# Transposes by strips through memory: the second layer's input in layer 0, and the query and key heads of three sequences, in a two-layer transformer kernel

## The chip, the cores and the metric

The kernel runs on one core of a Trainium2 chip, in one launch. The metric is the time on the device in microseconds (us). The kernel before takes 1124.99 us, the median of three runs (1124.24 to 1125.60). Everything is computed in 32-bit floats.

The engines are named as in the profile: PE (TensorE, matrix products; PEld is its loading of weights), DVE (VectorE), ACT (ScalarE), POOL (GpSimd) and SP (SyncE, which here only issues transfers). Each engine works through its own list of instructions in order, and waits in front of one whose inputs are not there. SP and ACT issue plain transfers (DMAs) in the same way, in order, POOL the gathers and scatters.

## The reference

`x` has 4 sequences of 1024 tokens with 256 features. Two layers follow each other:

```python
xn = _layernorm(x)
x = x + attention0(xn) + ffn0(xn)        # layer 0
xn = _layernorm(x)
x = x + attention1(xn) + experts1(xn)    # layer 1
```

- `attention0` is causal, one head, 256 wide: softmax(q kT / 16) v over all earlier tokens, then a layer norm of (out + v) and a projection. `ffn0` is relu(xn W1 + b1) W2 + b2, 1024 wide.
- `attention1` is a gated unit: `qk = silu(ln(xn) Wqk + bqk)` is 64 wide; four heads come of it by a scale, an offset and a rotation by position (`rope`): quad_q, lin_q, quad_k, lin_k. Within groups of 64 tokens, relu(quad_q quad_kT / 64 + bias) squared weighs `v`; beside it lin_q multiplies the sum over the sequence of lin_kT v, divided by n. Their sum is multiplied by a gate silu(ln(xn) Wg + bg), projected and normalised.
- `experts1` sends each token to the best 2 of 8 experts (softmax of xn Wg); each expert computes (silu(xn W1 + b1) * (xn W3 + b3)) W2 + b2, 512 wide, where W1, W2, W3 have low-rank corrections added. The two results are added with their weights.

## The kernel before

**Layer 0** runs in 16 units of 256 tokens, 4 per sequence (`u = 4b + p`; line 739 ff.). The iteration of unit `u` holds for PE: transposes of the nearest attention weights (`turns`, line 546), the first part of the hidden layer (`hidden`, `pm`, L539), the queries of unit u + 1 (L476), the transposes of `xl` of unit u - 1 (`norms_turn`, L636), the weighted sum `pz` (`weighted`, L571 near, L574 far), the logits of unit u - 1 (`pl`, L653), the scores of unit u + 1 (`sc`, L492), the rest of the hidden layer, then `finish` (`po` L590, `pv` L594), and a product of low-rank expert factors (`multiply`, L411 to L414), whose result is added to expert weights on DVE (L417) and stored by SP (`wm<-wt`, L418 and L420).

`xl` is the normalised input of layer 1, made on DVE by `norms` at the end of an iteration (L621). `norms_turn` makes `xlT` of it, with features on partitions: four PE transposes into PSUM and a copy by ACT (L641). Its products with the router's and the qk weights are made by `logits`. For sequences 1 to 3 SP stores `xlT` (`xld`) for later.

**Strips.** DVE can transpose blocks of 32 x 32, not across the 128 partitions. Some data is therefore turned by way of DRAM: it is stored, loaded again in four transfers of 32 partitions that bring the blocks to their places in runs of 32 numbers (128 bytes), and turned by one DVE instruction. The kernel before does so with `xn` of units above 2 (`strip`, lines 431 to 436, turned at L455) and with attention weights on tokens of earlier units. For the latter, `bands` (line 515) stores the weights of each half of a unit (`atd`, L519), loads the matching rows of `xn` in another order (`xn2`, L524, once per unit) and loads the weights as `band` (L529), turned at L566. They are called for units that are `far` (u > 1 and p > 0).

**Layer 1** begins with the attention of sequence 0 (about 500 to 560 us), then come 36 blocks of experts (32 of 256 tokens and 4 of 128, about 560 to 926 us), then the attention of sequences 1 to 3, with the gathers of the experts' results. In an experts' block PE runs `up` (32 products, L957) and, for the block before, `down` (16 products, L978). DVE makes `g` (L965), turns the next block's `xt` into `xT` (L945) and scales `yt` (L980). SP loads the weights of the block after next; `xt` comes through ACT's queue.

For a sequence of the attention, `heads` (line 1072) applies silu to `qk` on ACT and makes the four heads on DVE: per half sequence two instructions of 128x1024 (L1084, L1088) and six of 128x512 (L1097 to L1102), into `a.r`. `values` makes `v` (L1114, L1116, L1119). `groups` (line 1123) turns `a.r` by 16 PE transposes (L1134, L1135), copied by DVE (`qlT`, L1136) and ACT (`kkT`, L1137), and uses it: `plk` (L1143), `ps` (L1150), later `po` (L1207). `gated` makes gate and sum, `project` the projection (`pj`, L1232) and its norm, `combine` adds the experts' results (L1046).

**What sets the order.** A scheduler orders each engine's list from the order of the program and from its own estimates of when things are ready. `tc.issue_after(x)` keeps an instruction behind another one. `tile_pool`s are buffers, with `bufs` copies for each tag; a tile of a tag waits until the tile `bufs` earlier is no longer read.

Of the kernel before, what the change touches and what calls it, by code (L numbers as in the profile page):

```python
# [67 lines left out]
def block_kernel(ctx: ExitStack, tc: tile.TileContext, x, wq, wk, wv, wfc, w1, w2, wqk, wvl, wg,  # L68
# [107 lines left out]
    xnd = dram.tile([B * NP, 2 * P, D], F32, name="xnd")  # L176
    atd = dram.tile([B * NP, 2 * P, (NP - 1) * 2 * P], F32, name="atd")
    xld = [dram.tile([P, DC, N], F32, name=f"xld{b}") for b in range(B)]
# [59 lines left out]
    with ExitStack() as l0:  # L238
# [27 lines left out]
        early = act.tile([P, 3 * D], F32, tag="att", name="early", bufs=4)  # L266
# [126 lines left out]
        def merge(u, after):  # L393
# [13 lines left out]
            def multiply():  # L407
# [3 lines left out]
                nc.tensor.matmul(pa, f1[:, ts(c, P)], f1[:, D : D + HID], start=True, stop=True)  # L411
                nc.tensor.matmul(pb, f3[:, ts(c, P)], f3[:, D : D + HID], start=True, stop=True)
                for i in range(2):
                    nc.tensor.matmul(pc[:, i, :], f2[:, ts(2 * c + i, P)], f2[:, HID : HID + D],  # L414
                                     start=True, stop=True)
                for k, p in enumerate((pa, pb, pc.rearrange("p i d -> p (i d)"))):
                    nc.vector.tensor_tensor(wt[:, k, :], p, wt[:, k, :], ALU.add)  # L417
                nc.sync.dma_start(  # L418
                    out=wm13[e, :, 0:EB1].rearrange("p (k c w) -> p k c w", k=2, c=DC)[:, :, c, :], in_=wt[:, 0:2, :])
# [8 lines left out]
        def keep(u):  # L428
            nc.sync.dma_start(out=xnd[u].rearrange("(i p) d -> p i d", p=P), in_=xns[u])

        def strip(u):
            keep(u)
            w = strips[u] = act.tile([P, DC, 2 * P], F32, tag="strip", name="strip", bufs=1)
            src = xnd[u].rearrange("(i r) (c j a) -> j r c i a", r=32, c=DC, a=32)
            for j in range(4):
                nc.sync.dma_start(out=w[32 * j : 32 * j + 32].rearrange("r c (i a) -> r c i a", a=32), in_=src[j])


        def first(u):
# [9 lines left out]
            if u > 2:  # L449
                strip(u)  # L450
# [31 lines left out]
        def scores(u, qT):  # L482
            b, p = divmod(u, NP)
            atts = []
            for i in range(2):
# [11 lines left out]
                att = act.tile([P, N], F32, tag="att", name="att", bufs=4)  # L497
# [6 lines left out]
                if far(u):  # L504
                    bands(u, i, att)
# [9 lines left out]
        def bands(u, i, att):  # L515
# [10 lines left out]
            got = act.tile([P, N], F32, tag="att", name="band", bufs=4)[:, 0:w]  # L526
            src = there.rearrange("(i r) (j k) -> j r i k", r=32, j=4)
            for j in range(4):
                nc.sync.dma_start(out=got[32 * j : 32 * j + 32].rearrange("r (i k) -> r i k", i=4), in_=src[j])  # L529
            bands.got.append(got)  # L530

# [50 lines left out]
        def finish(u, hT, zT):  # L582
# [3 lines left out]
            for i in range(2):  # L586
# [6 lines left out]
                for c in range(DC):  # L593
                    nc.tensor.matmul(pv, zT[:, c, ts(i, P)], vo_s[:, c, :, :],  # L594
                                     start=(c == 0), stop=(c == DC - 1))
# [11 lines left out]
        def norms(u):  # L607
# [21 lines left out]
            return xl  # L629

        def norms_turn(u, xl):
            b, p = divmod(u, NP)
            pt = bank([P, DC, 2 * P], "pt")
            for i in range(2):
                for c in range(DC):
                    nc.tensor.transpose(pt[:, c, ts(i, P)], xl[:, i, ts(c, P)], ident)  # L636
# [4 lines left out]
            nc.scalar.copy(xlT, pt)  # L641
            if b:
                nc.sync.dma_start(out=xld[b][:, :, ts(p, 2 * P)], in_=xlT)
# [3 lines left out]
        def logits(u, xlT, lg):  # L647
# [3 lines left out]
            for i in range(2):  # L651
                for c in range(DC):
                    nc.tensor.matmul(pl[:, i, :], xlT[:, c, ts(i, P)], wqr_s[:, c, :],  # L653
                                     start=(c == 0), stop=(c == DC - 1))
# [77 lines left out]
        for u in range(U):  # L732
# [7 lines left out]
            if u == 1:  # L740
                for k in range(3):
                    keep(k)
                fold_second(raw)
# [17 lines left out]
            if u:  # L761
                xlT = norms_turn(u - 1, xl)
            zT = weighted(u, attT)
            if u:
                logits(u - 1, xlT, lgs)
# [18 lines left out]
            finish(u, hT, zT)  # L784
            if u + 1 < U:
# [20 lines left out]
    with ExitStack() as l1:  # L806
# [141 lines left out]
        def up(xT, w13, n):  # L948
            g = exp.tile([P, EC, n], F32, tag="g", name="g")
            for m2 in range(EC // 2):  # L950
# [9 lines left out]
                for j in range(2):  # L960
                    m = 2 * m2 + j
                    nc.scalar.activation(s[:, j, :], p1[:, j, :], AF.Silu, bias=w13[:, EB1 + m : EB1 + m + 1])  # L962
# [26 lines left out]
        def blocks(order, ahead):  # L989
            last = None  # L990
            xts, ws, xT = ahead
            for k, i in enumerate(order):
# [6 lines left out]
                if i == 3:  # L999
                    tokens.after = weights.last  # L1000
                    slots(up.g)
                    heads.after = up.g
                if k + 1 < len(order):
                    xT = turn(xts.pop(order[k + 1]), wide(order[k + 1]), up.early if i == 0 else None)
                if last is not None:
# [4 lines left out]
        def experts(ahead):  # L1010
# [7 lines left out]
            values.after = down.last  # L1018
# [52 lines left out]

        def heads(b):
            a = at[b]
            bt = ts(b, NT)
            with tc.issue_after(at[0].silu0 if b == 0 else at[0].link), tc.issue_after(route.exp):
                nc.scalar.activation(qk[:, bt, :], qk[:, bt, :], AF.Silu)
            a.r = mid.tile([P, NT, 4, QK], F32, tag="r", name="r")
            for h in range(NH):
                tt = slice(h * T, (h + 1) * T)
                nt = slice(b * NT + h * T, b * NT + (h + 1) * T)  # L1080
                shape = [P, T, 4, QK]
                hd = tmp.tile(shape, F32, tag="hd", name="hd")
                with tc.issue_after(heads.after) if b == 1 else nullcontext():
                    nc.vector.tensor_tensor(hd, qk[:, nt, :].unsqueeze(2).to_broadcast(shape),  # L1084
                                            hg_s[:, h].unsqueeze(1).to_broadcast(shape), ALU.mult)

                with tc.issue_after(a.pace[2]) if b == h == 0 else nullcontext():
# [294 lines left out]
```

## Time and profile before

| what | value |
|---|---|
| runs | 1124.99 us median (1124.24 to 1125.60) |
| profiled execution | 1128.42 us, of which the span from the first to the last instruction is 1126.7 |
| granted PE clock, mean | 0.998 of full speed |
| PE busy | 1106.9 us (98%) |
| DVE busy | 555.4 us (49%) |
| ACT busy | 288.7 us (26%) |
| plain transfers of SP (queue q1) | 137.89 MB, 37.9% of the 16 DMA engines' span |
| plain transfers of ACT (queue q10) | 18.10 MB, 7.5% |
| layer 0, 60 to 440 us | PE busy 380.00, DVE 184.16, DMA 0.45 |
| experts, 560 to 930 us | PE busy 369.64, DVE 141.53, DMA 0.69 |
| attention of sequences 1 to 3, 930 to 1127 us | PE busy 185.62, DVE 134.70, DMA 0.23 |

A line of the timeline gives start, length, engine, program line, operation, out<-in, shape, type and count. A PE record lasts from an instruction's start until its result is written; neighbours overlap, so the step from one start to the next is what an instruction takes in the queue. A line of the waits gives who waited for whom: us in total, times, longest.

### The profile page before, as it was taken

The numbers are of one execution on the slowest core, as the hardware profiler recorded it, in microseconds if no ns is written. First come the engines' busy times: TensorE is split into PE (matmuls) and PEld (weight loads), VectorE is DVE, ScalarE is ACT, GpSimd is POOL, SyncE is SP. The second block draws the span as 40 slices with busy tenths as digits, with TensorE's granted clock in tenths as the row PEclk, the third lists the DMA queues.
The fourth block names the chain that finished last, engine by engine and source line by source line (L and its number), as shares of the span: only waits on it lengthen the run. The fifth ranks groups of instructions, "written<-read, shape, count | busy, mean of one in ns | idle before, by whom it ended". The sixth has DMA issues, their size and how long they took to land. (4 is left out here: it accounts for less than half of the span.)

```text
span 1126.7 us, 15401 instructions
## 1 busy us (share of the span) xinstructions
PE 1106.9 (98%) x5132; PEld 867.4 (77%) x5132; DVE 555.4 (49%) x1533; ACT 288.7 (26%) x758; POOL 177.7 (16%) x216
## 2 busy tenths in 40 slices
PE   8999999999999999999999999999999999999997
PEld 6788888888888888774688888888888884655645
DVE  5444554455444454547575623322332326677946
ACT  3323333333323333225211111111111113121121
POOL 2200002222032114141000000000000004453410
PEclk9999999999999999999999999999999999999999
DMA  8735434553455334420648786777777621322301
GB/s 308 200 100 160 129 99 149 159 178 119 132 162 155 94 128 141 158 96 33 222 101 290 212 269 190 241 227 221 238 228 223 231 85 57 121 76 75 95 28 37
DMA packets 186801, 173.77 MB, mean 154 GB/s; under 512 B 113888, under 2 KB 156384, under 8 KB 181600
## 3 DMA queue, kind: packets, MB, share of 16 engines
q1 hardware_dynamic: 99216, 137.89, 37.9%
q10 hardware_dynamic: 81360, 18.10, 7.5%
q0 software_dynamic: 6144, 16.79, 4.5%
q8 instruction: 41, 0.67, 0.3%
q14 instruction: 40, 0.33, 0.1%
HBM read 122.78 MB, written 51.02 MB: 154 GB/s over the span
## 5 line engine op out<-in xcount | busy, mean ns | idle before, releaser
L957 PE MATMUL p<-xT,w 128*128 128x256 f32 (+1 forms) x1152 | 241.2, 368 | 0.0
L957 PEld LDWEIGHTS p<-xT,w 128*128 128x128 f32 x1152 | 209.4, 190 | 26.9 <-issue 0.3
L1036 POOL DMA_INDIRECT y<-yg,slot x64 | 65.3, 1021 | 491.0 <-DVE v L1116 421.2
L962 ACT ACTIVATE s<-p,w 128x256 f32<-128x256 f32 (+1 forms) x144 | 58.8, 459 | 314.3 <-PE p L957 228.4
L965 DVE SCALAR_TENSOR_TENSOR g<-p,w,s 128x256 f32<-128x256 f32 (+1 forms) x144 | 60.8, 463 | 159.1 <-PE p L957 156.8
L978 PE MATMUL py<-w,g 128*128 128x256 f32 x544 | 123.4, 379 | 0.0
L539 PE MATMUL pm<-xnT,w_s 128*128 128x256 f32 x512 | 118.5, 379 | 0.0
L590 PE MATMUL po<-w_s,hT 128*128 128x256 f32 x512 | 116.1, 380 | 0.0
L978 PEld LDWEIGHTS py<-w,g 128*128 128x128 f32 x544 | 102.9, 190 | 14.2 <-DVE g L965 0.3
L590 PEld LDWEIGHTS po<-w_s,hT 128*128 128x128 f32 x512 | 96.9, 190 | 20.1 <-issue 8.0
L539 PEld LDWEIGHTS pm<-xnT,w_s 128*128 128x128 f32 x512 | 95.6, 192 | 11.6
L714 POOL DMA_INDIRECT xg<-xr,put x64 | 63.9, 998 | 209.0 <-ACT hT L542 138.2
L492 PE MATMUL sc<-xnT,qT 128*128 128x256 f32 (+1 forms) x320 | 65.8, 361 | 0.0
L542 ACT ACTIVATE hT<-pm,colt 128x256 f32<-128x256 f32 x128 | 53.9, 466 | 42.2 <-PE pm L539 42.2
L1114 PE MATMUL pv<-wvl_s,xl 128*128 128x512 f32 x128 | 58.1, 599 | 3.4 <-DVE v L1116 3.1
L594 PE MATMUL pv<-vo_s,zT 128*128 128x512 f32 x128 | 60.1, 592 | 0.0
L1232 PE MATMUL pj<-wo_s,gd 128*128 128x256 f32 x256 | 57.0, 381 | 2.6 <-DVE o L1234 2.1
L492 PEld LDWEIGHTS sc<-xnT,qT 128*128 128x128 f32 x320 | 54.6, 191 | 6.0 <-ACT qT L479 0.2
L1185 PE MATMUL pg<-xl,wg_s 128*128 128x512 f32 x128 | 57.5, 593 | 0.0
L1232 PEld LDWEIGHTS pj<-wo_s,gd 128*128 128x128 f32 x256 | 48.0, 190 | 10.2 <-DVE o L1234 3.3
L980 DVE TENSOR_TENSOR yt<-py,w 128x512 f32<-128x512 f32 (+1 forms) x36 | 23.8, 662 | 59.0 <-PE py L978 59.0
L603 DVE SCALAR_TENSOR_TENSOR x<-pv,rs,x 128x256 f32<-128x256 f32 x32 | 15.5, 484 | 72.1 <-ACT rs L189 47.7
(256 smaller groups left out, 1351.8 us busy)
## 6 DMA issues: line engine op xcount, KB each, us to landing
w<-wm SPq DMA_DIRECT2D x36, 1028.0 KB
w<-wm SPq DMA_DIRECT2D x36, 640.0 KB
wt<-in_ew_dram SPq DMA_DIRECT2D x16, 768.0 KB
wm<-wt SPq DMA_DIRECT2D x16, 512.0 KB
xt<-xg ACTq DMA_DIRECT2D x128, 64.0 KB
yg<-yt ACTq DMA_DIRECT2D x32, 256.0 KB
xnd<-xn SPq DMA_DIRECT2D x16, 256.0 KB
wm<-wt SPq DMA_DIRECT2D x16, 256.0 KB
```

Source lines behind the costliest of these rows:

```text
L492: nc.tensor.matmul(sc[:, kp * 2 * P : kp * 2 * P + w], qT[:, c, ts(i, P)], xnTs[b * NP + kp][:, c, 0:w], start=(c == 0), stop=(c == DC - 1))
L539: nc.tensor.matmul(pm[:, j, :], w1_s[:, c, ts(2 * m2 + j, P)], xnTs[u][:, c, :], start=(c == 0), stop=(c == DC - 1))
L590: nc.tensor.matmul(po[:, i, :], hT[:, m, ts(i, P)], w2_s[:, m, :], start=(m == 0), stop=(m == IC - 1))
L594: nc.tensor.matmul(pv, zT[:, c, ts(i, P)], vo_s[:, c, :, :], start=(c == 0), stop=(c == DC - 1))
L714: w = nc.gpsimd.indirect_dma_start(out=xg, out_offset=bass.IndirectOffsetOnAxis(ap=put[:, b * NT + t : b * NT + t + 1], axis=0), in_=xrs[b ...
L957: nc.tensor.matmul(p[:, j, :], w13[:, w0 : w0 + P], xT[:, c, :], start=(c == 0), stop=(c == DC - 1))
L962: nc.scalar.activation(s[:, j, :], p1[:, j, :], AF.Silu, bias=w13[:, EB1 + m : EB1 + m + 1])
L965: up.g = nc.vector.scalar_tensor_tensor(g[:, m, :], p3[:, j, :], w13[:, EB3 + m : EB3 + m + 1], s[:, j, :], ALU.add, ALU.mult).ins
L978: down.last = nc.tensor.matmul(py[:, k, :], g[:, m, ts(k, P)], w2[:, m * D : (m + 1) * D], start=(m == 0), stop=(m == EC - 1)).ins
L1036: w = nc.gpsimd.indirect_dma_start(out=ys[b][:, t, k, :], out_offset=None, in_=yg, in_offset=bass.IndirectOffsetOnAxis(ap=slot[:, n : n + ...
L1114: nc.tensor.matmul(pv, a.xl[:, c, ts(t, P)], wvl_s[:, c, :], start=(c == 0), stop=(c == DC - 1))
L1232: nc.tensor.matmul(pj, a.gd[:, m, ts(n, P)], wo_s[:, m, :], start=(m == 0), stop=(m == HC - 1))
```

## The change

It has four parts.

1. **`xl` of sequences 0 to 2 (units 0 to 11) in strips.** `norms` stores `xl` in DRAM (`xlr`) and loads it in strips (`strip`, now for any tile). `norms_turn` turns it by one DVE instruction, kept behind the last scores of the iteration, in place of four PE transposes and an ACT copy. For the iterations u = 1 to 12 `norms_turn` and `logits` are called after `finish`, and `logits`' products come behind the last `pv`. Sequence 3 keeps the PE transposes.
2. **The heads of sequences 1 to 3** are made in the experts' blocks 5, 8, 11, 14, 17 and 20, half a sequence in each: silu behind that block's own (ACT), then the eight DVE instructions behind its `g`. ACT's queue stores the result (`rd`) in the next block. `heads_back` loads it in strips (`qs`, `ks`) and, for the linear keys, plainly (`rl`): ten loads of SP per sequence, those of sequence 1 behind the last expert weights. `groups` turns them by three DVE instructions in place of 16 PE transposes and four copies.
3. **Stores behind the fetches of attention weights.** The stores of `xn`, `xld` and `wm13` are kept behind the last `band` fetch issued so far (`bands.last`). `multiply`'s products are kept behind the last `pv`.
4. **Buffers.** The four buffers of `att`, which `band` shared, become two of `att` and two of `band`; `strip` has two buffers in place of one; the pools of the last stage stand in another order, and one of them (`tmp`) is gone.

```diff
-        def strip(u):
-            keep(u)
-            w = strips[u] = act.tile([P, DC, 2 * P], F32, tag="strip", name="strip", bufs=1)
-            src = xnd[u].rearrange("(i r) (c j a) -> j r c i a", r=32, c=DC, a=32)
+        def keep(there, rows):
+            with tc.issue_after(bands.last) if bands.last else nullcontext():
+                nc.sync.dma_start(out=there.rearrange("(i p) d -> p i d", p=P), in_=rows)
+
+        def strip(there, rows):
+            keep(there, rows)
+            w = act.tile([P, DC, 2 * P], F32, tag="strip", name="strip", bufs=2)
+            src = there.rearrange("(i r) (c j a) -> j r c i a", r=32, c=DC, a=32)
             for j in range(4):
                 nc.sync.dma_start(out=w[32 * j : 32 * j + 32].rearrange("r c (i a) -> r c i a", a=32), in_=src[j])
+            return w
...
                 for k, p in enumerate((pa, pb, pc.rearrange("p i d -> p (i d)"))):
                     nc.vector.tensor_tensor(wt[:, k, :], p, wt[:, k, :], ALU.add)
-                nc.sync.dma_start(
-                    out=wm13[e, :, 0:EB1].rearrange("p (k c w) -> p k c w", k=2, c=DC)[:, :, c, :], in_=wt[:, 0:2, :])
+                with tc.issue_after(bands.last) if bands.last else nullcontext():
+                    nc.sync.dma_start(
+                      out=wm13[e, :, 0:EB1].rearrange("p (k c w) -> p k c w", k=2, c=DC)[:, :, c, :], in_=wt[:, 0:2, :])
                 nc.sync.dma_start(out=wm2[e, :, ts(c, HID)], in_=wt[:, 2, :])
...
-            got = act.tile([P, N], F32, tag="att", name="band", bufs=4)[:, 0:w]
+            got = act.tile([P, (NP - 1) * 2 * P], F32, tag="band", name="band", bufs=2)[:, 0:w]
...
+            return strip(xlr[u], xl) if b < B - 1 else xl
...
-            nc.scalar.copy(xlT, pt)
+            if b < B - 1:
+                with tc.issue_after(scores.last):
+                    nc.vector.transpose(xlT, xl)
+            else:
+                pt = bank([P, DC, 2 * P], "pt")
+                for i in range(2):
+                    for c in range(DC):
+                        nc.tensor.transpose(pt[:, c, ts(i, P)], xl[:, i, ts(c, P)], ident)
+                nc.scalar.copy(xlT, pt)
...
             finish(u, hT, zT)
+            if u and late:
+                logits(u - 1, norms_turn(u - 1, xl), lgs, finish.last)
...
+                for keep in kept:
+                    keep()
+                kept = []
+                if others and k > 3 and k % 3 == 2:
+                    kept.append(heads_ahead(*others.pop(0)))
                 if last is not None:
                     down(*last)
...
+        def heads_ahead(b, h):
+            nt = slice(b * NT + h * T, b * NT + (h + 1) * T)
+            with tc.issue_after(up.silu):
+                nc.scalar.activation(qk[:, nt, :], qk[:, nt, :], AF.Silu)
+            r = exp.tile([P, T, 4, QK], F32, tag="r", name="r")
+            half_heads(b, h, exp, exp, r, up.g)
+
+            def keep():
+                nc.scalar.dma_start(out=rd[b][ts(h, T * P), :].rearrange("(t p) f -> p t f", p=P),
+                                    in_=r.rearrange("p t i d -> p t (i d)"))
+            return keep
...
+        def heads_back(b):
...
+            for j in range(4):
+                turned(a.qs, slice(0, N), j, 32 * j)
+            for h in range(NH):
+                for j in (0, 1) if h else (2, 3):
+                    turned(a.ks, ts(h, T * P), j, P + 32 * j)
+                f = P if h == 0 else P + QK
+                fetch(out=rl[:, h * T : (h + 1) * T, :],
+                      in_=rd[b][ts(h, T * P), f : f + QK].rearrange("(t p) f -> p t f", p=P))
...
+            else:
+                for h in range(NH):
+                    a.pace.append(nc.vector.transpose(qlT[:, ts(h, T * P)], a.qs[:, ts(h, T * P)]).ins)
+                nc.vector.transpose(kkT, a.ks)
```

`half_heads` holds the eight DVE instructions that `heads` held. In the order that the scheduler makes of the changed program, the far products `pz` (L574 before) stand later in PE's list in several units: in units 5, 6 and 10 between the scores of the next unit, in unit 3 behind three of the `po`, and in units 7 and 11 behind all 16 of them, directly ahead of the four `pv`.

## The prediction

> **What bounds the kernel now.** I read the page first (busy time, slices), then busy time by stretch, then the timeline of the places that the diff touches, then who TensorE waited for.
>
> The page, part 1 and three rows of part 2:
>
> ```profile
> PE 1106.9 (98%) x5132; PEld 867.4 (77%) x5132; DVE 555.4 (49%) x1533; ACT 288.7 (26%) x758; POOL 177.7 (16%) x216
> ...
> PE   8999999999999999999999999999999999999997
> ...
> DVE  5444554455444454547575623322332326677946
> ...
> DMA  8735434553455334420648786777777621322301
> ```
>
> TensorE (PE) is busy in 1106.9 of 1126.7 us and dips only at both ends. So a matmul taken off its queue is time, and a new wait of PE is time. The stretches (us, then busy time of PE, PEld, DVE, ACT, POOL; clock, DMA share, GB/s):
>
> ```profile
> 60.00:440.00 380.00, 380.00 (x1832) 310.87 (x1833) 184.16 (x578) 123.78 (x384) 69.96 (x64) 1.00 0.45 136
> ...
> 560.00:930.00 370.00, 369.64 (x1765) 324.66 (x1763) 141.53 (x312) 59.40 (x145) 0.00 (x0) 1.00 0.69 212
> 930.00:1127.00 197.00, 185.62 (x767) 109.03 (x766) 134.70 (x326) 41.19 (x68) 65.34 (x64) 1.00 0.23 70
> ```
>
> In layer 0 (60 to 440) and in the experts (560 to 930) PE has no gap, and DVE has half and more of the time free; in the tail (sequences 1 to 3 of the second attention) PE idles 11.4 us and DVE is at 68%.
>
> **What a PE transpose costs.** In unit 7's iteration:
>
> ```profile
> 239.94 0.60 PE L636 MATMUL pt<-ident,xl 128*128 128x128 f32 x4
> 240.38 0.82 PE L571 MATMUL pz<-attT,xn 128*128 128x256 f32 x4
> ```
>
> Four transposes of xl hold PE's queue from 239.94 to 240.38: 0.44 us, 0.11 each. Their own records last longer (0.275 in the costliest groups by form), because neighbours overlap. In the tail:
>
> ```profile
> 940.77 0.27 PE L1134 MATMUL pq<-ident,r 128*128 128x128 f32 x1
> 940.88 0.27 PE L1135 MATMUL pk<-ident,r 128*128 128x128 f32 x1
> ...
> 942.61 0.65 PE L1143 MATMUL plk<-v,r 128*64 128x512 f32 x2
> ```
>
> Sixteen take 1.84 us. The Trainium skill ("TensorE: Matmul & The Clock Gate", part 4 on the PE-mode transpose) prices one at about 390 ns alone and 275 ns within a kernel. The change removes 48 (xl, 12 units) and 48 (pq/pk, 3 sequences): by the page's 275 ns that were 26.4 us, by the starts in the trace 48 x 0.11 + 3 x 1.84 = 5.3 + 5.5 = **10.8 us**. I take the trace: a record's length is latency, the step from start to start is what the next matmul waits.
>
> **Part 1: xl through DRAM (units 0 to 11).** PE: -5.3 us, and ACT's copy (12 x 0.60) goes, beside PE. DVE gains 12 transposes of the form of L455 (128x512, 0.71): 8.5 us in 380 of which it has 196 free: hidden. The router's 8 products (0.85 us of PE) move to the end of the iteration and cost the same; one small routing chain on DVE moves with them. SP gets one store (0.39) and four strip loads (0.62 each, like L436's pairs of 1.24) per unit: 2.9 us of issue, in a unit of 24 to 33 us.
>
> The DMA rule speaks against it: the skill ("DMA: Bandwidth & Descriptors", Specifications) wants 512 bytes or more per transfer, below which the DMA engine reads, modifies and writes; these strips run in 128-byte pieces. At worst the 256 KB read counts double: 0.77 MB a unit with the store, some 4.4 us at the 175 GB/s that the trace shows at 200 to 250, in a unit of 30 us whose DMA engines are 45 to 58% busy. Taken as a rate it costs nothing by the rule or by the row; what can cost is the queue.
>
> *Queue.* SP's order in the changed kernel puts `wm2<-wt`, which waits for the DVE additions of the last unit's product, between `atd<-att` and the four `band<-atd` of the second half in units 3, 6, 7, 10 and 11. Behind it stand those four fetches; for them wait a DVE transpose and then PE's `pz` on xn2. In unit 6 of the present kernel the iteration starts at 200.19 (end of pv) and the last addition ends at 204.17, so +4.0; the moved routing operations add up to 1 us. Then wm2 0.4, four fetches 1.73 (the profiled four at 228.05), some 2 us to land (a store and the load behind it stand 2.6 us apart at 219.72 and 222.33), a transpose 0.7: ready at +9.3 to +10.5. PE wants it, by the new order (pz's far half now behind part of `sc`), at about +9.5 in unit 6, +8.6 in unit 10 and +10.8 in unit 3. So 0 to 1 us, 0.7 to 2 us and 0 to 0.5 us of new waits: I take **+2.0** in all (0 to 4). Units 5 and 9 have no wm2 in front: 0.
>
> *Units 7 and 11.* Here the order on PE puts all 12 far `pz` behind the last `po`, and pv directly behind them; on DVE both `x<-po` additions stand ahead of the second band's transpose. So after the last po PE waits for an addition (0.43), a 768-wide transpose (0.95) and two semaphores (some 0.1): 1.5 us. Then pv waits for `zT<-pz` (0.69 and 0.2): 0.9 us, which po's matmuls cover today. 2 x 2.4 = **+4.8**. Nothing else is queued that could fill it. In unit 3 nine po stand between pz and the second pv, five before the first (over 1 us): covered.
>
> Part 1 sums to -5.3 + 2.0 + 4.8 = +1.5.
>
> **Part 2: the heads of sequences 1 to 3.** PE: -5.5. On DVE a half sequence costs 2 x 1.22 + 6 x 0.69 = 6.6 us, now in six of 36 experts' blocks (10.3 us of PE each, in which DVE does some 3.9). That is 10.5 in the loaded block, spread into the next: DVE lags and recovers. `hd` (1.22) stands ahead of `xT`'s transpose: it ends some 3.0 us after up's end instead of 1.75; PE needs it after down's 16 products, 3.45 us after. Slack 0.4: 0 (0 to 0.5 each). It is gone after a 128-wide block, where down takes half; the six blocks then wait 0 to 1. `r`'s store goes through ACT's queue, which is free five sixths of the time. Ten loads per sequence (4 qs, 4 ks, 2 rl at 0.4 to 0.6: 5 us of SP) come with the last w2 loads for sequence 1: the last ks lands near 919, the products wanting it run at 926. Costed +0.5 (0 to 4).
>
> In the tail DVE loses 3 x 13.2 of head work and two qlT copies (0.69) per sequence, and gets three transposes of 0.69 per sequence: -37 us of its 134.7. PE's waits there:
>
> ```profile
> PE pv L1114 <- DVE v L1116: 3.1, 4, 1.3
> PE pj L1232 <- DVE o L1234: 2.1, 2, 1.8
> ...
> PE po L1207 <- DVE gd L1213: 0.5, 1, 0.5
> ```
>
> The gd wait (1025.61, right behind `hd` on DVE) and part of pv's go: -2.5 of 5.7 (-1 to -5). The 1.8 us wait of pj sits between two projections that keep their order and loses 16 transposes of filler near it: +0.5 (0 to 1.5). Part 2: -5.5 + 0.5 - 2.5 + 0.5 = -7.0.
>
> The new pools, the split of `att` into att and band and the second strip buffer reuse less memory across stages: no wait in the present trace names them; 0, their danger is inside the range of the band's wait.
>
> **Sum.** 1.5 - 7.0 = -5.5. The profiled execution took 1128.4 us (span 1126.7 and 1.7 around it), so one like it would take 1122.9. The runs' median is 1124.99, 3.4 lower; the same difference gives 1119.5. I forecast **1119.5**.
>
> **Rivals.**
> - *Bands and strips are late everywhere* (slower). SP serves in order; each xl round trip adds a store and a load that must wait for it, 2.6 us, in front of or between atd, xn2 and band. For it: the loads stand among those in units 2, 3, 6, 7, 10 and 11, and no idle PE shows how close today's are. Against: loads for xl are mostly queued in the first third, atd's second half two thirds later. If each of six units waits one round trip more, 6 x 2.6 = 15.6, less the 2.0 counted: 1133. It turns the result when the extra waits pass 5.5 us, 0.9 per unit.
> - *No stalls beyond those today* (full gain). DVE is under half busy and the orders in 7 and 11 may leave less than 2.4 us; with all new waits of part 1 gone: -5.3 - 7.0, so 1112.7; half of them, 1116.
> - *DVE and the queues pinch the experts.* Six blocks with 10.5 us of DVE against 10.3 of PE, the DMA at 0.69, 3 MB more stored and read: if xT comes 1 us late in each of six and the qs for sequence 1 hold up DVE's last g by 2: 8 less 0.5 counted, eating the gain: 1127; half of it, about 1123.5. For it: qlT's two transposes stand ahead of the last block's g. Against: qs land near 909 and are wanted at 914.
> - *The change does nothing*: only if PE's transposes were hidden; the start-to-start step in a queue without gaps excludes it.
>
> **How the numbers follow.** Chances: my sum 0.45 (its own range 1116 to 1122.5), full gain 0.23, pinched experts 0.14 (half faster or level, half slower), late bands 0.18. A measurement tells 0.2%, 2.25 us, from nothing. Faster 0.45 + 0.23 + 0.03 = 0.71; same 0.08; slower 0.21. The range from the full gain's 1112 to partly late bands, 1129, leaves out about a tenth on either side.
>
> **What would show it.** Right: PE 96 instructions of transposes fewer and 10 to 11 us less busy; idle PE of about 2.4 us in units 7 and 11, released by DVE attT or x and then zT; in the tail no wait behind hd. Step by step: a wait of PE pz on the band's DMA or attT in units 3, 6, 10 sizes the queue; up's first product waiting on xT, or py on g, in the six blocks sizes the heads. Wrong: idle PE of over 1 us in most layer-0 units, a gap before 930, or pv and pj waiting as long as now.

## The result, and the profile after

The changed kernel takes 1140.47 us (median of four runs, 1139.49 to 1142.55), the kernel before 1124.97 on the same chip: ratio 1.014 (95% interval 1.0123 to 1.0158). It is 15.5 us slower where I forecast 5.5 faster; the time lies outside my range (1112 to 1129).

The page of the changed kernel, its first part and three rows of the slices:

```profile
PE 1101.0 (97%) x5036; PEld 861.8 (76%) x5036; DVE 565.5 (50%) x1548; ACT 281.9 (25%) x743; POOL 172.5 (15%) x216
...
PE   8999999997999989999999999999999999999997
...
DVE  5344456444554337545865454454532333394856
...
PEclk9999999998999989999999999999999999999999
```

The 96 matmuls are gone, but PE's row now dips to 7 and 8 in two places, and the granted clock's row dips at both. They lie in layer 0, as busy time by stretch shows (us; PE, PEld, DVE, ACT, POOL; clock, DMA share, GB/s):

```profile
60.00:440.00 380.00, 358.72 (x1675) 292.20 (x1674) 180.58 (x532) 115.41 (x357) 61.88 (x56) 0.98 0.50 143
...
560.00:930.00 370.00, 368.44 (x1791) 319.39 (x1790) 168.93 (x381) 61.11 (x149) 0.00 (x0) 1.00 0.75 231
930.00:1138.00 208.00, 201.18 (x820) 121.64 (x818) 121.41 (x311) 40.67 (x69) 61.65 (x64) 0.99 0.33 90
```

PE had no gap between 60 and 440 us; now 21.3 us are idle there, and the clock averages 0.98. DVE was busy 184.16 us of this stretch and is busy 180.58: it did not become full. What PE waited for, over the whole span (us in total, times, longest):

```profile
PE pl L671 <- DVE xlT L651: 12.7, 2, 7.4
PE pz L585 <- DVE attT L577: 4.8, 3, 2.0
...
PE pv L605 <- DVE zT L588: 1.6, 2, 0.8
...
PE po L601 <- DVE x L607: 1.2, 2, 0.6
```

The two largest are the router's products `pl` (L671, before L653), waiting for the `xlT` that DVE turns. In the kernel before, `pl` stood amid the iteration and did not wait:

```profile
247.09 1.01 PE L653 MATMUL pl<-wqr_s,xlT 128*128 128x72 f32 x8
```

PE's timeline of the changed kernel from unit 7 on shows one of the two, and in front of it the waits that I had forecast for units 7 and 11:

```profile
248.81 3.72 PE L601 MATMUL po<-w_s,hT 128*128 128x256 f32 x16 [0.59 <-DVE x L607]
253.94 2.86 PE L585 MATMUL pz<-attT,xn 128*128 128x256 f32 x12 [1.40 <-DVE attT L577]
...
260.82 3.70 PE L605 MATMUL pv<-vo_s,zT 128*128 128x512 f32 x8 [0.78 <-DVE zT L588]
...
273.03 1.98 PE L671 MATMUL pl<-wqr_s,xlT 128*128 128x72 f32 x8 [7.44 <-DVE xlT L651]
...
275.02 3.62 PE L550 MATMUL pm<-xnT,w_s 128*128 128x256 f32 x8
...
278.72 1.89 PE L550 MATMUL pm<-xnT,w_s 128*128 128x256 f32 x8
```

After 7.44 us without work, eight `pm` take 3.62 us; eight more of the same, 3.7 us later, take 1.89. The stretches there say why (the seventh figure after the span is the clock):

```profile
266.00:273.00 7.00, 0.00 (x0) 0.00 (x0) 6.94 (x27) 3.37 (x12) 1.26 (x1) 0.67 0.00 0
273.00:275.00 2.00, 1.97 (x9) 1.97 (x10) 0.00 (x0) 0.00 (x0) 0.00 (x0) 0.50 0.43 141
...
277.00:279.00 2.00, 2.00 (x8) 1.51 (x8) 0.08 (x1) 0.32 (x1) 0.00 (x0) 0.61 0.94 305
279.00:281.00 2.00, 2.00 (x11) 1.77 (x10) 0.96 (x2) 0.86 (x3) 0.98 (x1) 1.00 0.04 13
```

While PE stands still, DVE is busy 6.94 of 7 us, with 27 instructions. DVE's timeline, some of them:

```profile
263.91 0.48 DVE L614 SCALAR_TENSOR_TENSOR x<-pv,rs,x 128x256 f32<-128x256 f32 x1 [2.53 <-ACT rs L192]
...
266.49 0.67 DVE L421 TENSOR_TENSOR wt<-pab,wt 128x512 f32<-128x512 f32 x1
...
269.76 0.70 DVE L632 TENSOR_SCALAR xl<-x,mean,rstd 128x256 f32<-128x256 f32 x2
...
270.47 0.72 DVE L185 BATCH_NORM_STATS2 st<-x 128x6 f32<-128x256 f32 x2
...
271.97 0.39 DVE L185 BATCH_NORM_STATS2 st<-x 128x6 f32<-128x256 f32 x1
272.28 0.69 DVE L651 STREAM_TRANSPOSE xlT<-strip 128x512 f32<-128x512 f32 x1
```

The transpose does not wait for its strips: DVE comes to it without a pause, and the last of the four strip loads, issued from 250.98 us on, had landed at 256.97, 15.3 us earlier. It stands in DVE's list behind the residual additions, the additions to the expert weights, the next `xl`, and the statistics of eight tiles of the next sequence, which fall due only in the last iteration of a sequence. (In unit 3 they fall due too, but there the transpose stands ahead of them, at 139.85 us, and PE does not wait.) PE needs it at once, because `pl` stands at the head of PE's next iteration.

The starts of the iterations (by the first low-rank product) tell where the time went. Layer 0, in us:

| iteration | before | after | in it |
|---|---|---|---|
| u2 to u6 | 152.5 | 152.4 | unit 5: 0.72, `sc` on `qT` |
| u7 | 29.9 | 31.9 | 0.59 + 1.40 + 0.78 = 2.77 |
| u8 | 26.3 | 36.8 | wait 7.44, half clock behind it 2.6 |
| u9 | 30.1 | 31.9 | 2.04, `pz` on `attT` |
| u10 | 33.1 | 32.6 | nothing |
| u11 | 29.9 | 31.9 | 2.77 |
| u12 | 26.3 | 34.0 | wait 5.30, half clock behind it 2.0 |
| u13, u14 | 64.1 | 64.5 | nothing |

(The half clock: from `pl`'s start to the next `qk_s` products takes 7.42 and 6.73 us in u8 and u12, against 4.78 at full clock, which is 5.85 in the units without a wait, less the 1.07 of the low-rank products that stand between there.) Unit 15 starts 23.1 us later than before (23.8 by the table, less 0.6 gained before unit 2). The waits add up to 12.74 + 5.54 + 2.04 + 0.72 = 21.0 us, the clock to 4.6, and 5.3 us of transposes are saved: 20.3; 2.8 are not accounted for. From there to the experts +0.2. The experts: 353.06 against 353.07 us. From the tail's first `pv` to its last `pj` group 179.14 against 190.72: -11.6. In all +11.7, as the spans (1138.5 and 1126.7) say. The other 3.8 us of the 15.5 are that the profiled execution before was 3.4 above its runs' median, and the one after is 0.3 below its own. (By chip the kernel before has medians from 1124.97 to 1128.06 us in the runs below, so every ratio here is taken on one chip.)

PE's waits in the changed kernel's tail:

```profile
PE pv L1186 <- DVE v L1188: 0.9, 1, 0.9
PE pj L1309 <- DVE o L1311: 0.4, 1, 0.4
```

PE is busy 177.51 us of the 179.14, against 185.25 of 190.72: 7.7 less work and 3.8 less idle time.

### The profile page after: what moved, and what is told of

Same layout as the page of the kernel before. It is cut to its first block, busy times and chain, and to the rows that moved or that the text cites. A ratio compares the mean times of both kernels' runs of the same rounds, so it can differ in the third digit from the quotient of the medians.

```text
span 1138.5 us, 15317 instructions
## 1 busy us (share of the span) xinstructions
PE 1101.0 (97%) x5036; PEld 861.8 (76%) x5036; DVE 565.5 (50%) x1548; ACT 281.9 (25%) x743; POOL 172.5 (15%) x216
## 5 line engine op out<-in xcount | busy, mean ns | idle before, releaser
L1063 POOL DMA_INDIRECT y<-yg,slot x64 | 61.7, 963 | 487.8 <-DVE v L1188 420.8
L550 PE MATMUL pm<-xnT,w_s 128*128 128x256 f32 x512 | 122.3, 386 | 0.0
L610 ACT ACTIVATE sq<-pv 128x256 f32<-128x256 f32 x32 | 12.3, 383 | 162.7 <-PE pv L605 162.7
L1002 DVE TENSOR_TENSOR yt<-py,w 128x512 f32<-128x512 f32 (+1 forms) x36 | 23.8, 660 | 51.1 <-PE py L1000 51.1
```

The source lines that it names most:

```text
L550: nc.tensor.matmul(pm[:, j, :], w1_s[:, c, ts(2 * m2 + j, P)], xnTs[u][:, c, :], start=(c == 0), stop=(c == DC - 1))
L1063: w = nc.gpsimd.indirect_dma_start(out=ys[b][:, t, k, :], out_offset=None, in_=yg, in_offset=bass.IndirectOffsetOnAxis(ap=slot[:, n : n + ...
```

## The experiments

My theory after the result: `pl` waits because `xlT`'s transpose is late in DVE's list, not because data is late; the half clock is a second price of long waits; part 2 is a gain. The rivals: the strips come late (the queue), and the clock falls for another reason than the wait.

**The two parts alone.** The first kernel keeps parts 2 to 4 and gives all units their PE transposes back; the second (its diff is not shown) is the kernel before with the changes to layer 0 alone, the order of the stores and the buffers there included.

```diff
  (e1_part2, against the changed kernel)
-            return strip(xlr[u], xl) if b < B - 1 else xl
+            return xl
...
-            if b < B - 1:
-                with tc.issue_after(scores.last):
-                    nc.vector.transpose(xlT, xl)
-            else:
+            if True:
                 pt = bank([P, DC, 2 * P], "pt")
...
-            late = u <= U - NP
```

> The changed kernel with part 1 undone: xl is turned by PE in all units again, and the router's products stand where they stood before; heads among the experts, store order and buffers as changed. The traces put +23 us on layer 0 and -11.5 us on the rest. Theory (part 1 alone costs): 1111 to 1116, some 11 below the kernel before, no stall of PE in layer 0. Rival (the new buffers and the order of the stores cost in layer 0 too): PE idle stays in layer 0, 1120 or more.

> The kernel before with only the changes to layer 0 (xl in strips, late logits, store order, buffers); heads of all sequences as before. Theory (the two parts add up): some 1125 + 23 = 1148, to 1152, with the waits of the router's products on xlT, 7.4 and 5.3 us, in units 7 and 11. Rival (the parts get in each other's way): near 1135.

Part 2 alone: 1122.77 us against 1127.79 before, ratio 0.9962 (0.9948 to 0.9976). Part 1 alone: 1153.16, ratio 1.0225 (1.0208 to 1.0242), with the same waits in layer 0 as the changed kernel to 0.02 us (7.44, 5.31, 2.03, twice 2.77). In `e1_part2`, which keeps the stores' order and the buffers, PE is busy in all of 60 to 440 us as before. So the loss is part 1's, and part 2 adds nothing to it. Part 2's tail takes 184.3 us in its profile, 5 more than in the changed kernel; so 1122.77 lies above the 1111 to 1116 that I had expected, though layer 0 has no stall. PE's timeline and one stretch of part 2 alone:

```profile
991.53 3.39 PE L1303 MATMUL pj<-wo_s,gd 128*128 128x256 f32 x8 [2.13 <-DVE o L1305]
```

```profile
992.00:994.00 2.00, 2.00 (x7) 1.56 (x6) 0.75 (x4) 0.00 (x0) 0.69 (x1) 0.50 0.48 135
```

A wait of `pj` that the changed kernel's trace does not have (its 0.4 is the whole), and half clock behind it. PE and DVE have the same orders there in both kernels. Of the fourteen profiles shown or told of here, seven have it (1.8 to 4.3 us, once with no releaser named), seven don't. In these seven DVE itself stands idle in front of an `o<-pj`, for 2.8 to 5.4 us; in `e1_part2`:

```profile
991.05 0.42 DVE L1305 TENSOR_TENSOR o<-pj,rowt 128x256 f32<-128x256 f32 x1 [3.16 <-remote]
```

PE's products recorded before it end at 989.39, so both engines stand idle from there to 991.05, and the profile names nothing that they wait for (`remote` is only its word for a releaser that it doesn't show); the cause stays open. With what follows it, the wait may be worth about 5 us: by that much the two tails differ, and the two ratios together would make 1.0186 of the whole change, which took 1.014 without it.

**Moving single positions.** `e3_order` holds the `po` products back behind the last far `pz`, to take away the waits of units 7 and 11. `e4_turn_order` besides holds the residual addition `x<-pv` behind `xlT`'s transpose (`after` is that transpose, which `norms_turn` now issues ahead of `finish`).

```diff
  (both)
                 for m in range(IC):
-                    nc.tensor.matmul(po[:, i, :], ...)
+                    with tc.issue_after(weighted.last) if far(u) else nullcontext():
+                        nc.tensor.matmul(po[:, i, :], ...)
  (e4_turn_order besides)
-                nc.vector.scalar_tensor_tensor(xt, pv[:, 1, :], rs, xt, ALU.mult, ALU.add)
+                with tc.issue_after(after) if after else nullcontext():
+                    nc.vector.scalar_tensor_tensor(xt, pv[:, 1, :], rs, xt, ALU.mult, ALU.add)
```

> The changed kernel with po held behind the last far pz in units with bands, so that the far products stand ahead of po in units 3, 7 and 11 as before. In the DVE list of this program xlT's transpose then stands ahead of the additions to the expert weights and of the statistics of the next sequence. Theory (the waits of 7.4 and 5.3 us are DVE's list alone): they shrink to under 2.5 us each, the 2.8 us at pz and pv in each of units 7 and 11 vanish: 1140.5 - 5.5 - 12 = about 1123. Rival (the strips of xl land late): the waits on xlT stay above 4 us, then with a DMA as the cause of DVE's idle time: 1132 or more.

> As the run before it, and x<-pv is held behind xlT's transpose in the units whose logits are late, so that the transpose stands ahead of both x<-pv and of all that follows. Theory: no wait of the router's products is left beyond 0.5 us, PE does not fall to half clock, 1140.5 - 5.5 - 17 = 1117 to 1120. Rival (strips land late): DVE stalls in front of xlT, and with it x and the next iteration: 1130 or more.

1135.01 us (1.0076, 1.0057 to 1.0094) and 1133.81 (1.0039, 1.0026 to 1.0053), both against 1127.79. The wait of `pl` shrinks to 1.28 in the first and is gone in the second. The strips are fetched no earlier (in unit 7 of `e3_order` 18.7 us after the iteration's start, in the changed kernel 18.4), so that settles that data was not late. But `pz` now waits for its bands, 2.86, 1.81 and 2.85 us (3.03, 1.81 and 2.86). PE's timeline of `e3_order`, unit 7:

```profile
247.38 2.86 PE L585 MATMUL pz<-attT,xn 128*128 128x256 f32 x12 [2.86 <-DVE attT L577]
```

Here 2.86 us did not cost the clock (12 products in 2.86 us, as elsewhere); in unit 11 of the same execution a wait of 2.85 did (clock 0.50 from 372 to 374 us, 0.66 to 376). The 20 runs of `e4_turn_order` differ in the same way: seven lie at 1127.2 to 1129.4 us with a mean clock of 0.997 to 0.999, most others at 1132 to 1136.6 with 0.989 to 0.994.

**Is the half clock due to the wait?** Twelve products of 128x256 (24 in the records), of no use to the result, are put into both waits; the low-rank products move ahead of them.

```diff
+            if u in (2 + NP, 2 + 2 * NP):
+                pw = bank([P, D], "pw")
+                with tc.issue_after(merge.pc):
+                    for _ in range(12):
+                        after = nc.tensor.matmul(pw, ident, w2_s[:, 0, :], start=True, stop=True).ins
```

> The changed kernel with 12 matmuls of 128x256 (some 5.2 us of PE) put between the products pc and pl at the ends of units 7 and 11, into a PSUM tile that nobody reads: they lie inside the waits for xlT and fill most of them. Theory (PE's clock falls to half in a wait of this length, and the slow matmuls behind it are part of the loss, 2.6 + 2.0 us): pl still starts when xlT is there, but granted clock stays 1.00 and pl and pm run at full speed: 4 to 5 us below the changed kernel. Rival (what follows a wait is slow for another reason, memory or queues): as the changed kernel, within 1 us.

1136.28 us against 1125.03, ratio 1.009 (1.0073 to 1.0107), where the changed kernel had 1.014. PE's timeline in units 7 and 11, then the stretches behind:

```profile
272.59 1.95 PE L676 MATMUL pl<-wqr_s,xlT 128*128 128x72 f32 x8 [2.16 <-DVE xlT L651]
...
397.82 5.45 PE L672 MATMUL pw<-w_s,ident 128*128 128x256 f32 x24
403.29 1.08 PE L676 MATMUL pl<-wqr_s,xlT 128*128 128x72 f32 x8
```

```profile
273.00:275.00 2.00, 2.00 (x11) 1.91 (x11) 0.37 (x2) 0.20 (x1) 0.00 (x0) 0.50 0.69 236
...
404.00:408.00 4.00, 4.00 (x24) 3.54 (x24) 1.42 (x4) 1.11 (x3) 0.64 (x1) 1.00 0.56 165
```

In unit 11 useless work fills the wait, the clock stays at 1.00, and iteration u12 takes 32.0 us instead of 34.0. In unit 7 the filler was too short: 2.16 us of idle time were left, and the clock fell as it did after 7.44. So in these two places the clock follows the wait, and in unit 11 the drop costs 2 us apart from it. (In unit 9 the new order puts a wait of 0.7 us in place of the 2.04.)

**Leaving the crowded units out.** Units 2, 6 and 10, whose `xlT` is wanted in the crowded iterations, keep their PE transposes (`e6_exempt`); or they keep the strips, and their `pl` are issued an iteration later (`e7_defer`).

```diff
  (e6_exempt, the same condition in norms and in norms_turn)
-            return strip(xlr[u], xl) if b < B - 1 else xl
+            return strip(xlr[u], xl) if b < B - 1 and p != 2 else xl
...
-            late = u <= U - NP
+            late = u <= U - NP and u % NP != NP - 1
  (e7_defer)
+            if u and owed:
+                logits(*owed)
...
-            if u and late:
+            if u and late and p < NP - 1:
                 logits(u - 1, norms_turn(u - 1, xl), lgs, finish.last)
+            owed = (u - 1, norms_turn(u - 1, xl), lgs) if u and late and p == NP - 1 else None
```

> The changed kernel with the third unit of each sequence (2, 6, 10) left as before: its xl is turned by PE in units 3, 7 and 11, and the router's products stand amid those iterations; nine units keep the strips. PE's list then has the far pz ahead of po in units 7 and 11 again. Theory (the loss sits in units 7 and 11, by order): their waits of 2.8 + 7.4 and 2.8 + 5.3 us and the half clock vanish; layer 0 comes to some 9 x 0.44 = 4.0 us less than before plus up to 2.5 in unit 9; with part 2's gain in the tail, 6 to 11 us: 0.6 to 1.2% below the kernel before. Rival (strips cost wherever they are, through SP's queue): layer 0 stays slower than before by 3 us or more.

> The changed kernel with the router's products of units 6 and 10 issued in the next iteration, behind its queries, in place of the end of iterations 7 and 11: xl is still turned through strips on DVE in all 12 units, and the far pz stay behind po in units 7 and 11. Theory (the product at the head of the next iteration is what makes a late xlT cost): 12.7 us of waits and 4.6 of slow clock go, the 2.8 us in each of units 7 and 11 stay: 17 us below the changed kernel, or level with the kernel before within 4 us. Rival (xlT comes so late that whoever uses it waits): 8 us or less below the changed kernel.

1126.55 us (1.0006, 0.9995 to 1.0017) and 1131.65 (1.0047, 1.003 to 1.0063), both against 1125.03. `e6_exempt` has no `pl` wait, and PE's list has the far `pz` ahead of `po` in units 7 and 11 again; but `pz` waits 3.8 and 3.4 us for the bands in units 7 and 11, and twice 0.5 for the routing chain in units 5 and 9. So three units give back nearly all of the loss, and what is left again stands in the same two iterations. In `e7_defer` the wait goes from unit 8, and one like it appears where no unit had it:

```profile
330.02 1.95 PE L671 MATMUL pl<-wqr_s,xlT 128*128 128x72 f32 x8 [5.39 <-DVE xlT L651]
```

I had not expected this: in unit 10's iteration the products had not waited before. At the head of an iteration another unit is hit as soon as DVE's list falls otherwise.

**Following the bands.** `e8_exempt_route` is `e6_exempt` with the routing chain an iteration later. `e9_wm2_behind` besides keeps the store `wm2` behind the last band fetch. `e10_loads_behind` does so with the loads of the experts' weights and low-rank factors too.

```diff
  (e8)
             if p == 0 and b:
-                routed = route(b - 1, lgs)
+                held_lg = lgs
...
+            if p == 1 and b:
+                routed = route(b - 1, held_lg)
  (e9 besides)
-                nc.sync.dma_start(out=wm2[e, :, ts(c, HID)], in_=wt[:, 2, :])
+                with tc.issue_after(bands.last) if bands.last else nullcontext():
+                    nc.sync.dma_start(out=wm2[e, :, ts(c, HID)], in_=wt[:, 2, :])
  (e10 besides: the loads of lt and wt in merge likewise)
```

> As the run with the third units exempt, and the routing chain of a finished sequence traced one iteration later, behind the far pz's transposes of unit 5, 9 and 13, so that DVE's list has less of it ahead of the bands. Theory (in unit 9 the 2.0 us are DVE's list, filled by the moved routing chain): that wait shrinks by 1 us or more, total 1 to 2 us below the exempt kernel. Rival (the band's data come late there): same as the exempt kernel.

> The run with exempt units and moved routing, and the second store of the expert weights (wm2) kept behind the last band fetch, as wm13 is. The loads of the next expert weights (wt, 768 KB) still stand ahead of the second half's four fetches on SP. Theory (in units 7 and 11 the band's data come late because SP's queue holds them behind wm2, which waits for DVE): the fetches go out 6 us earlier or more and the waits of 4.4 and 3.5 us at the far pz are gone or under 1 us, the half clock with them: 10 us below the run before, some 1113. Rival (the load of wt, which waits for the queries' ACT, holds them as well): no gain, 1121 to 1125.

> As the run before it, with the loads of expert weights and factors (wt, lt) kept behind the last band fetch too. Theory: nothing that waits stands ahead of the band fetches in units 3, 6, 7, 10 and 11, except a load of x in unit 7; the waits at the far pz in units 7 and 11 shrink to what DVE's list leaves (its transpose stands behind the scores' softmax), under 2 us, total 1112 to 1117. Rival (the fetches are slow by themselves, runs of 128 bytes): the waits stay at 3 us and more.

`e8`: 1123.48 us against 1125.03, 0.9986 (0.9974 to 0.9998). The small waits of units 5 and 9 are gone. In unit 7, SP's queue, DVE and PE:

```profile
233.71 0.36 SPq L425 DMA_DIRECT2D wm<-wt  x1
234.16 0.61 SPq L406 DMA_DIRECT2D wt<-in_ew_dram  x1
234.86 1.98 SPq L539 DMA_DIRECT2D band<-atd  x4
```

```profile
242.96 0.98 DVE L577 STREAM_TRANSPOSE attT<-band 128x768 f32<-128x768 f32 x1 [1.40 <-DMA band<-atd]
```

```profile
243.99 5.28 PE L585 MATMUL pz<-attT,xn 128*128 128x256 f32 x12 [4.42 <-DVE attT L577]
```

This is the mechanism of my queue step: `wm2`'s store waits for DVE's additions, a load of 768 KB goes out behind it, and the band behind both lands (at 242.0 us, as far as the trace has it) late enough that DVE waits 1.40 us for it and PE 4.42.

`e9`: 1121.73 us against 1124.97, 0.9971 (0.996 to 0.9982). The fetch is issued 9.75 us earlier, and PE still waits 2.93. SP's queue, then DVE:

```profile
225.11 1.73 SPq L540 DMA_DIRECT2D band<-atd  x4
```

```profile
241.20 0.35 DVE L510 TENSOR_SCALAR att<-att,rinv 128x256 f32<-128x256 f32 x1
241.47 0.97 DVE L578 STREAM_TRANSPOSE attT<-band 128x768 f32<-128x768 f32 x1
```

The band had landed by about 230.5 us. The transpose stands in DVE's list behind the softmax of the next unit's scores, which waits for PE and ACT several times: an order again, not data and not a full engine.

`e10`: 1126.83 us against 1124.97, 1.0016 (1.0006 to 1.0025), worse by 5 us. With the two loads out of the way, another stands in front, and goes out only at 239 us:

```profile
239.07 0.40 SPq L88 DMA_DIRECT2D x<-in_x_dram  x1
239.56 2.29 SPq L542 DMA_DIRECT2D band<-atd  x4
```

`pz` of unit 7 then waits 8.72 us. I had expected a gain, or waits as long as before.

**The last order.** `e11_band_first` is `e9` with the additions of the causal mask, the start of the softmax, kept behind the bands' transposes in the iterations of units 7 and 11, where `scores` makes those of units 8 and 12. `e12_part2_again` is the kernel of `e1_part2` on the same chip: the difference of the two in layer 0 is what strips in nine units are worth when nothing waits (the two also differ in the place of `wm2`, of the routing chain and of the mask).

```diff
-                nc.vector.tensor_tensor(sc[:, ts(t, P)], sc[:, ts(t, P)], causal, ALU.add)
+                with tc.issue_after(weighted.turn) if u % NP == 0 and u > NP else nullcontext():
+                    nc.vector.tensor_tensor(sc[:, ts(t, P)], sc[:, ts(t, P)], causal, ALU.add)
```

> The run with wm2 behind the fetches, and on DVE the transposes of both bands put ahead of the next unit's first softmax instruction in units 7 and 11. There the band's data have landed long before, and the transpose stood behind two softmax chains: 2.9 us of wait at the far pz, and some 1.6 us of half clock behind it. Theory (what was left is DVE's list and the clock): both vanish, 2 x 4.5 = 9 us below the run before: some 1113, about 1% below the kernel before. Rival (the softmax, held back, delays the scores' way through ACT and atd, and the next unit waits instead): 1118 to 1122.

> Part 2 alone once more, beside the run before it on the same chip, as the yardstick for it: 5 us below the kernel before, as it was. If the strips of xl are worth anything once nothing waits for them (9 units x 0.44 = 4 us), the run before this one must be faster than this one by about 4 us, unless the tail differs; if not, part 1 has no gain to give.

`e11`: 1118.42 us (1117.44 to 1121.10) against 1128.06, ratio 0.9919 (0.9904 to 0.9933). `e12`: 1124.00, 0.9964 (0.995 to 0.9977), as `e1` had it. DVE and PE of `e11` in unit 7, then its layer 0:

```profile
236.61 1.83 DVE L579 STREAM_TRANSPOSE attT<-band 128x768 f32<-128x768 f32 x2
239.62 0.30 DVE L503 TENSOR_TENSOR sc<-sc,causal 128x128 f32<-128x128 f32 x1 [1.18 <-PE sc L500]
```

```profile
240.29 2.75 PE L587 MATMUL pz<-attT,xn 128*128 128x256 f32 x12
```

```profile
60.00:440.00 380.00, 379.79 (x1822) 312.22 (x1821) 193.98 (x598) 123.47 (x385) 70.18 (x64) 1.00 0.51 150
```

No wait in unit 7, and PE is full in layer 0 at full clock. From u1's start to the experts `e11` takes 521.9 us and `e12` 526.4: 4.5 us for nine units, where nine times the prediction's 0.44 us are 4.0. The strips' runs of 128 bytes cost PE nothing that shows, at a DMA share of 0.51 against 0.45. This kernel beats `e12`, and lies 9.6 us below the kernel before, with the 3.6 us wait of `pj` still in its profiled tail. 1118 is the rival's number and not the theory's 1113, but the rival's sign, a wait of the next unit, does not show in layer 0; the tail of `e11` is 5.6 us longer than that of `e9`, which has no such wait.

## Why the prediction was wrong

By its steps, in the order of the prediction:

- **PE transposes, -5.3 in part 1:** right. `e11` against `e12` measured 0.50 us per unit for the 0.44 read from starts. The 275 ns each of the Trainium skill ("TensorE: Matmul & The Clock Gate", Part 4: PE-mode transpose; where its lone 390 ns is for bf16 data) would have made 1.1 per unit.
- **"12 transposes of DVE: hidden" and "the router's 8 products move to the end of the iteration and cost the same":** this step failed, and decided the sign. I compared 8.5 us of DVE with 196 us of its free time in the stretch. Free time in a stretch does not say where in the list an instruction stands. Two of the twelve stood behind a pile of other work, and the moved products had been put where PE meets them first: 7.4 + 5.3 us, with 4.6 us of half clock behind them. The order of PE and DVE in the changed kernel could be read beforehand; I read PE's in units 7 and 11, and DVE's only around the bands, not at the end of the iteration behind them.
- **The band behind `wm2`, +2.0 in units 3, 6 and 10:** no wait showed in any of the three. Unit 9, put at nothing, waited 2.04 us: DVE's routing chain, moved with the products ("one small routing chain moves"), stood ahead of the second band's transpose; with that transpose ahead of most of it (`e6`) 0.5 us was left, and with the chain an iteration later (`e8`) nothing. The queue mechanism exists (`e8` to `e9`), but in the changed kernel PE's order, with `pz` late, covers it.
- **Units 7 and 11, 2 x 2.4:** right in mechanism and nearly in size, 2 x 2.77. The clock did not fall there.
- **Price of a wait:** missing from the sum. Every wait was counted at its length; behind the two long ones the half clock cost 4.6 us more.
- **Part 2, -7.0:** the sign was right, the size depends on the tail's `pj` wait. Heads in the experts' blocks: +0.5 predicted, nothing measured (353.06 against 353.07), so the pinched rival falls. The tail was put at -7.5; it came to -6.4 with that wait (`e1`) and -11.6 without it. In the second case PE's busy time fell by 7.7 where 5.5 were counted, and its idle time by 3.8 where 2.0 were. The 2.2 more of busy time I cannot place.
- **The 3.4 us between profile and median:** carried over to the changed kernel; there it is 0.3. This took 3 us off my number by itself; no run shows where the 3.4 came from.

With the measured terms the sum of part 1 becomes -5.3 + 0.7 + 2.0 + 5.5 + 12.7 + 4.6 = +20.2, instead of +1.5, and no gain in the tail makes that up. The slower rival (late bands and strips) had the sign and its turning point of 5.5 us, but the wrong cause: nothing was late in the changed kernel's queues; the transposes stood late on DVE. Its 1133 also left out the clock.

Left open: the `pj` wait in the tail, 2.8 us of layer 0, and 2.2 us of the tail's busy time.

## What to carry to other kernels

Where a step is to be hidden on another engine, follow that engine's list from the instruction back to its inputs in the most crowded iteration; its busy share in the stretch says only that a place exists, not that the instruction stands in it. If the consumer moves to the head of an iteration, its input must be ready by then in every unit, and one crowded unit in four was enough to lose the gain of all. Where PE waits two microseconds or more, a run at half clock may follow and belongs in the price. When one wait is mended look at the same place again: here each order that was tried uncovered the next wait, and only the last one beat part 2 alone.

## What the runs showed of the hardware that I had not expected

- The clock can fall after short waits. The Trainium skill ("TensorE: Matmul & The Clock Gate", Part 1: The HAM clock gate) has half clock after an idle window of about 3.4 us, and the window runs free, so that the phase matters. Here idle times of 2.13 us (tail of `e1`) and 2.16 us (`e5`) were enough, 2.15 us (tail of `e12`) and 2.04 us (unit 9) were not, and in `e3` 2.86 us was not and 2.85 was. That length alone does not decide fits the page's free window; that two microseconds are already at risk does not fit its figure, and the measurement decides. The half clock lasted from 3.4 us (`e1`, 992.0 to 995.4) to 6.8 us (`e5`, 272.5 to 279.4) of work. From `pl` to `qk_s` it cost 2.6 us after the wait of 7.44, 2.0 after 5.30 and 3.2 after 2.16 (`e5`, 8.01 against 4.78), so the longer wait did not make it dearer.
- A wait is not needed for it. In `e7` the clock fell with PE busy all the time:

```profile
290.00:292.00 2.00, 2.00 (x7) 0.49 (x5) 0.38 (x1) 0.88 (x4) 0.00 (x0) 1.00 0.00 0
292.00:294.00 2.00, 2.00 (x14) 1.63 (x12) 1.47 (x7) 0.59 (x3) 0.00 (x0) 1.00 0.00 0
294.00:296.00 2.00, 2.00 (x7) 1.59 (x7) 1.93 (x11) 0.96 (x4) 0.00 (x0) 0.61 0.03 8
```

The same shows in `e3` (0.61 from 392 to 394 us) and `e4` (0.51 from 394 to 396). In all three `pl` stands between the low-rank products just before, some 3.1 us of small products in a row. The changed kernel has that order too at the end of unit 3 (141.1 to 144.3 us) without a drop; whether it has a part in it no run here tests.

- The times of one kernel can fall into groups with the granted clock, without any change: `e4_turn_order`'s 20 runs span 9 us. Its profiled execution has half clock after waits of 3.03 and 2.86 us in layer 0 and 4.33 in the tail.
- In a queue that serves in order a fetch waits for whatever waits in front of it: taking two loads away from there (`e10`) let a third stand there, and PE waited 8.72 us instead of 2.93.
